# Layer 1 of a four-layer image network: 14 pieces of 224 pixels instead of 19 of 166, and two samples' statistics taken inside it

## The chip, the core and the metric

The kernel runs on one core of one Trainium2 chip. The core has a matrix engine (TensorE, "PE" in the profile, whose weight loads the profile lists apart as "PEld"), a vector engine (DVE), an activation engine (ACT), a general engine (POOL) and a queue engine (SP) that issues transfers. The metric is the device time of one launch in microseconds, as a median of several runs. All data is float32.

## What is computed

The input is 8 images of 128 channels and 56 x 56 = 3136 pixels. Four layers follow each other, each of the form `x = x + layer(groupnorm(x))`. Layer 0 is a windowed attention, layer 2 a masked convolution, layer 3 a residual block of two 3 x 3 convolutions. The change is in layer 1, a recurrent network that walks over the pixels of each image in order:

```python
seq = jnp.transpose(xn, (0, 2, 3, 1)).reshape(B, H * W, C)
inp = tanhshrink(jnp.einsum('blc,ic->bli', seq, w_in) + b_in)
xgate = jnp.einsum('bli,hi->blh', inp, w_ih) + b_ih + b_hh
def step(h, xg):
    h_new = jnp.tanh(xg + h @ w_hh.T)
    return (h_new, h_new)
_, hs = jax.lax.scan(step, h0, xgate_t)
out_seq = jnp.einsum('blh,oh->blo', outputs, w_out) + b_out
```

The sizes are 128 channels, 256 inner inputs (`RIN`), and a state of 512 (`RH`). Layer 2 then needs, for each sample, the mean and variance of every group of 4 channels over all 3136 pixels of layer 1's result, before it can normalise that sample.

## The kernel before

All 8 images stay on the chip in one tile `X` of 128 partitions (channels) by 8 x 3136 pixels. The layers update it in place.

**Layer 1 is cut along the pixels.** The state forgets quickly, so the 3136 steps of a sequence are cut into `NCH` = 19 pieces of `TC` = 166 pixels that advance together: one step handles one pixel of every piece of every image, 19 x 8 = 152 columns. As 19 x 166 = 3154, the first piece is short by `LEAD` = 18 pixels. Each piece begins from the state that its predecessor has at its end, which isn't known at the start. So `WARM` = 56 steps come first, over the last 56 pixels of every piece, from a zero state; the state that they leave, moved on by one piece (`first`, L925 to L930), is where the real run begins. The real run then takes `TC` steps. There are `END = WARM + TC` = 222 steps, issued in pairs by the loop at L906.

**One step** (`step`, L847) does two products per block of 128 state channels, `KH` = 4 blocks. The input product (`wih`) takes 4 x 2 = 8 matmuls, the recurrent one (`whh`) 4 x 4 = 16; all are issued at L858. Each has its own 128 x 128 weights. A float32 matmul leaves two records of a weight load and two of a matmul in the trace, and this document counts records. The result `ps` comes in two halves `f` of two blocks. ACT takes the tanh of each into `hs[f]` (L881). The matmuls of the next step that read `hs[0]` come ahead of those that read `hs[1]`.

**Three phases** follow from that loop:

- warming, 56 steps: input product, recurrent product. The input product of these steps, with its bias, is also copied out of PSUM (`gk`, L870) and stored in DRAM (`kept`, L871).
- main run, `TC` - 56 = 110 steps: input product, recurrent product, and per pair the output product `po` (L893).
- recall, 56 steps: the pixels of the warm steps come again, so their input product isn't computed again but fetched (`recall`, L841), added by DVE (`v`, L884) and given to ACT (L885). These steps have the recurrent product and `po` only.

**Around the steps**, `prepare` (L814) makes the normalised input of a pair of pixels: `xn` on POOL (L822, L826), one product `pi` of two matmuls (L833), tanh on ACT (L835) and `inp` on DVE (L836). `outputs` (L887) forms `po` by four matmuls over a pair of pixels: its first two are issued just ahead of the next pair's first step, its last two ahead of that pair's second step, and then DVE adds the result into `X` (L899). `pi` and `po` work on two pixels at once, thus on 304 columns. The order of the matmuls is written out by hand (a manual schedule of PE); a scheduler places the other engines' work.

**Between the layers.** After the loop POOL compares the states at the seams of the pieces (L936 to L946, into `held`), whose outcome decides at the very end whether layers 1 to 3 are redone by a plain sequential version (L1295; this isn't executed here). In `convolutions` (L953), statistics of sample 0 are seven `bn_stats` over 448 pixels each (L1010) and a `bn_aggr` (L1012); two small products (`pm`, L1016, and `pv`, L1028), a root (L1032) and a reciprocal (L1038) follow, then the normalised image is written into a padded tile (L1040), and `spread` copies it into a tile `g3` by ACT and by transfers on SP and POOL (L1057, L1059). The first product of layer 2 (L1069) reads `g3`. The statistics of sample 1 are one `bn_stats` ahead of that normalisation and six behind it. SP also issues the loads of layer 2's weights there (L982 to L993, L1092), ahead of its share of L1059.

Of the kernel before, what the change touches and what calls it, by code (L numbers as in the profile page):

```python
# [10 lines left out]
F32 = mybir.dt.float32  # L11
# [3 lines left out]
ALU = mybir.AluOpType  # L15
# [3 lines left out]
P = 128  # L19
B = 8  # L20
HW = 56
NPX = HW * HW
# [4 lines left out]
BLK = NW * WPX  # L27
NBLK = NPX // BLK
# [3 lines left out]
KI, KH = RIN // P, RH // P  # L32
PW = HW + 2
EPS = 1e-5
NCH = 19
TC = 166
LEAD = NCH * TC - NPX
WARM = 56
CL = P // 4
VECTORS = (("gamma", 1), ("beta", 1), ("b_in", KI), ("b_ih", KH), ("b_hh", KH), ("b_out", 1))  # L40
# [4 lines left out]
def conv_stack_kernel(ctx: ExitStack, tc: tile.TileContext, a: dict, out: bass.AP):  # L45
# [3 lines left out]
    nc = tc.nc  # L49

    const = ctx.enter_context(tc.tile_pool(name="const", bufs=1))
# [5 lines left out]
    X = xpool.tile([P, B, NPX], F32, name="X")  # L57
# [10 lines left out]
    for b in range(2, B):  # L68
        nc.sync.dma_start(X[:, b, :], a["x"][b])
    mv1 = const.tile([P, B, 2], F32, name="mv1")  # L70
    root = const.tile([P, 1], F32, name="root")
    vecs = const.tile([P, 14], F32, name="vecs")
    eps = const.tile([P, 1], F32, name="eps")
# [44 lines left out]
    broken = keep.tile([1, 1], I32, name="broken")  # L118
    held = keep.tile([P, KH * (NCH - 1) * B // 16], F32, name="held")
    between = ExitStack()  # L120
    samp = between.enter_context(tc.tile_pool(name="samp", bufs=2))
    with ExitStack() as l0:
# [35 lines left out]
        for i in range(3):  # L158
            t = c0.tile([P, WS, PW], F32, name=f"vrow{i}", tag=f"vrow{i}")
# [10 lines left out]
        qs, ks, selrs, v3s, lepes, os_, st1, norms = {}, {}, {}, {}, {}, {}, {}, {}  # L170
# [378 lines left out]
        stats, mean, var = measure(0)  # L549
# [54 lines left out]
        for b in range(1, B):  # L604

            at = [FIRST + i // 4 for i in range(NBLK)] if b == 1 else [pair_of(b - 2, 0) + i for i in range(NBLK)]
# [6 lines left out]
            at = [pair_of(b - 1, i * NW) - 6 for i in range(NBLK)]  # L613
            if b == 1:
                at = [max(t, 2 + 2 * i) for i, t in enumerate(at)]
# [15 lines left out]
        for p in range(FIRST, END + 6):  # L631
            ready = [t for t in jobs if t[1] <= p and all(placed.get(k, p) < p for k in t[7])]
            light, long = (next((t for t in ready if t[5] == k), None) for k in (LIGHT, LONG))
            ready = [t for t in ready if t[5] == ONE]
# [36 lines left out]
        with tc.manual_schedule(engines={ET.PE, ET.Activation, ET.DVE, ET.Pool}):  # L671
            for p in range(FIRST, END + 6):
# [12 lines left out]
                for W in (2 * p - 2, 2 * p - 1):  # L685
                    b, w = divmod(W, NWIN)
# [49 lines left out]
    with ExitStack() as l1:  # L736
# [5 lines left out]
        at = np.cumsum([0] + [n for _, n in VECTORS])  # L742
        gamma, beta, bin_, bih, bhh, bout = (vecs[:, lo:hi] for lo, hi in zip(at, at[1:]))
# [16 lines left out]
        t = c1.tile([P, B], F32, name="t1")  # L760
# [16 lines left out]
        scl = keep.tile([P, B], F32, name="scl")  # L777
        nc.vector.tensor_scalar(scl, r, rb, None, ALU.mult)
        ctr = keep.tile([P, B], F32, name="ctr")
# [6 lines left out]

        pre.close()  # L790
        fast = ExitStack()
        row = fast.enter_context(tc.tile_pool(name="row", bufs=2))
# [2 lines left out]

        def pieces(t):

            c = 0 if t >= LEAD else 1
            at = c * TC + t - LEAD
            return c, X[:, :, at : at + (NCH - 1 - c) * TC + 1 : TC].rearrange("p b c -> p c b")  # L800

        kept = dram.tile([WARM, P, KH, NCH, B], F32, name="kept")

        def pixel(s):

            return TC - WARM + s if s < WARM else s - WARM

        def known(s):

            return s - TC if s >= TC else None  # L810

        seam = row.tile([P, KH, NCH - 1, B], F32, name="seam", bufs=1)

        def prepare(s):  # L814

            xn = row.tile([P, 2, NCH, B], F32, name=f"xn_{s}", tag="xn")
            engine = nc.gpsimd if s else nc.vector
            for t in range(2):
                c, src = pieces(pixel(s) + t)
                if c:  # L820
                    engine.memset(xn[:, t, :c], 0.0)
                engine.tensor_tensor(  # L822
                    xn[:, t, c:], src,
                    ctr.rearrange("p (o b) -> p o b", o=1).broadcast_to((P, NCH - c, B)), ALU.subtract,
                )
                engine.tensor_tensor(  # L826
                    xn[:, t, c:], xn[:, t, c:],
                    scl.rearrange("p (o b) -> p o b", o=1).broadcast_to((P, NCH - c, B)), ALU.mult,
                )
            inp = row.tile([P, KI, 2, NCH, B], F32, name=f"inp_{s}", tag="inp")  # L830
            for m in range(KI):
                pi = ps_a.tile([P, 2, NCH, B], F32, name=f"pi_{s}_{m}", tag="pi")
                nc.tensor.matmul(pi, win_t[:, m * P : (m + 1) * P], xn, start=True, stop=True)  # L833
                th = row.tile([P, 2, NCH, B], F32, name=f"th_{s}_{m}", tag="th")
                nc.scalar.activation(th, pi, AF.Tanh, bias=bine[:, m : m + 1])  # L835
                nc.vector.scalar_tensor_tensor(  # L836
                    inp[:, m], pi, bine[:, m : m + 1], th, ALU.add, ALU.subtract,
                )
            return inp
# [47 lines left out]
        def outputs(s, hs):  # L887

            po = ps_a.tile([P, 2, NCH, B], F32, name=f"po_{s}", tag="po")

            def part(ks):
                for k in ks:
                    nc.tensor.matmul(po, wout[:, k, :], hs[k // 2][:, :, k % 2], start=(k == 0), stop=(k == KH - 1))  # L893

            def end():
                part((2, 3))
                for t in range(2):
                    c, dst = pieces(pixel(s) + t)
                    nc.vector.scalar_tensor_tensor(dst, po[:, t, c:], bout, dst, ALU.add, ALU.add)  # L899

            return [lambda: part((0, 1)), end]

        with tc.manual_schedule(engines={mybir.EngineType.PE}):
            END = WARM + TC
            x, prev, todo = prepare(0), None, []
            for s in range(0, END, 2):  # L906
                hs = [row.tile([P, 2, 2, NCH, B], F32, name=f"hs{f}_{s}", tag=f"hs{f}", bufs=3) for f in range(2)]
                for t in range(2):
                    if known(s) is not None:
                        x = recall(s + t)  # L910


                    if todo:
                        todo.pop(0)()
                    step(s + t, x, hs if t else prev, hs)
                    if t == 0 and s + 2 < END and known(s + 2) is None:
                        nxt = prepare(s + 2)
                if pixel(s) + 2 == LEAD and s >= WARM:
                    for f in range(2):
                        nc.gpsimd.memset(hs[f][:, 1, :, 0, :], 0.0)  # L920
                x, prev = nxt, hs
                if s >= WARM:
                    todo = outputs(s, hs)
                if s + 2 == WARM:
                    first = [row.tile([P, 2, 2, NCH, B], F32, name=f"first{f}", tag=f"hs{f}", bufs=3) for f in range(2)]  # L925
                    for f in range(2):
                        nc.vector.tensor_copy(first[f][:, 1, :, 1:, :], hs[f][:, 1, :, : NCH - 1, :])
                        nc.gpsimd.memset(first[f][:, 1, :, 0, :], 0.0)
                        nc.gpsimd.tensor_copy(seam[:, 2 * f : 2 * f + 2], hs[f][:, 1, :, : NCH - 1, :])
                    prev = first  # L930
            for part in todo:
                part()

# [17 lines left out]
    def convolutions(held=None):  # L953

        with ExitStack() as l2:
            c2 = l2.enter_context(tc.tile_pool(name="c2", bufs=1))
            few = l2.enter_context(tc.tile_pool(name="few", bufs=2))
# [43 lines left out]
            class Norm:  # L1001


                def __init__(self, b, name):
                    self.b, self.name = b, name
                    self.mv = few.tile([P, 2], F32, name=f"mv_{name}", tag="mv2", bufs=3)
                    self.st = few.tile([P, NBLK, 6], F32, name=f"st_{name}", tag="st2")

                def stats(self, i):
                    nc.vector.bn_stats(self.st[:, i, :], X[:, self.b, i * BLK : (i + 1) * BLK])  # L1010
                    if i == NBLK - 1:
                        nc.vector.bn_aggr(self.mv, self.st.rearrange("p i s -> p (i s)"))  # L1012

# [119 lines left out]

            ET = mybir.EngineType
            weights, verdict = [], None
            norms = [Norm(b, f"l2_{b}") for b in range(2)]
            with ExitStack() as order:
                if held is not None:
                    order.enter_context(tc.manual_schedule(engines={ET.PE, ET.Activation, ET.DVE, ET.Pool}))
# [14 lines left out]
                for n in range(B * NBLK):  # L1154
                    b, i = divmod(n, NBLK)
# [86 lines left out]
            def prepare(b):  # L1242

                end = {}
                mv = small.tile([P, 2], F32, name=f"mv3_{b}", tag="mv")

                def norm():
                    gm, r = group_norm(b, ps_g, "pg", f"l3_{b}", mv)
                    nc.vector.tensor_scalar(
                        pad3[:, 1 : 1 + HW, 1 : 1 + HW], X[:, b, :].rearrange("p (u v) -> p u v", v=HW),  # L1250
                        gm, r, ALU.subtract, ALU.mult,
                    )
                    end.update(shift(b, gm, r))

                half = HW // 2
                sums = lambda y: column_sums(va, slice(1 + y, 1 + y + half), pad3[:, 1 + y : 1 + y + half, :])
                stats = lambda: channel_stats(b, mv, f"l3_{b}")
                return end, [stats, norm, lambda: sums(0), lambda: sums(half)]
# [258 lines left out]
```

## Time and profile before

| | us |
|---|---|
| median of 3 runs (3682.0 to 3686.88) | 3684.55 |
| the profiled execution's own time | 3677.05 |
| its span | 3675.1 |
| PE busy (share of the span) | 3545.7 (96%) |
| PE weight loads busy | 2914.9 (79%) |
| DVE busy | 1889.8 (51%) |
| ACT busy | 1654.2 (45%) |
| POOL busy | 1349.3 (37%) |
| first and last recurrent or input matmul of layer 1 begin at (L858) | 1408.9 and 2933.2 |

The span runs from the first to the last instruction of the profiled execution; the 1.95 us around it are launch and end. The profiled execution was 7.5 us faster than the median of the runs. A line of the profile that names a group gives the source line, the engine, the operation, the tile written and those read, the shapes and the count, then the busy time and the mean duration of one. Busy time counts overlapping instructions once, so it is less than count times duration where they are pipelined.

### The profile page before, as it was taken

Reading aid. Unit: us, or ns where it says so; the run is one execution under the profiler, and the core shown is the slowest. Engines: PE = TensorE matmul, PEld = TensorE weight load, DVE = VectorE, ACT = ScalarE, POOL = GpSimd, SP = SyncE. Lnnn points to the kernel's source line nnn. Section 1 sums busy time; section 2 is a strip of 40 time slices with the busy share of each in tenths; the row PEclk is TensorE's granted clock in tenths of the full one; section 3 lists DMA queues with packets and bytes.
Section 4 is the critical chain, followed back from the end, with each engine's and each line's share of the span. In section 5 each row is a group of like instructions: output and inputs, shape, how many; then the busy total and the mean of one; then the engine's idle time right before and its main releaser. Section 6 shows DMA issues by size and latency. Waiting matters only on the chain.

```text
span 3675.1 us, 85966 instructions
## 1 busy us (share of the span) xinstructions
PE 3545.7 (96%) x30150; PEld 2914.9 (79%) x30150; DVE 1889.8 (51%) x3923; ACT 1654.2 (45%) x5149; POOL 1349.3 (37%) x3663
## 2 busy tenths in 40 slices
PE   5999999999999998999999999999999989999998
PEld 3666666666666667999999999999999833799998
DVE  5888888888878773222111111111122266757665
ACT  2787878888888883222222222222211154122222
POOL 3767667676766662111111111111000066323221
PEclk8999999999999999999999999999999999999999
DMA  5444444343434431111000000000022166100000
GB/s 208 108 107 108 110 104 107 100 117 101 118 102 114 122 93 57 49 45 49 21 1 1 1 1 1 1 1 1 18 59 59 45 168 169 34 23 23 31 21 34
DMA packets 195814, 241.74 MB, mean 66 GB/s; under 512 B 42480, under 2 KB 153520, under 8 KB 194352
## 3 DMA queue, kind: packets, MB, share of 16 engines
q1 hardware_dynamic: 160992, 125.99, 11.8%
q0 software_dynamic: 32576, 109.48, 11.3%
q8 instruction: 245, 4.01, 0.5%
q14 instruction: 193, 1.58, 0.2%
q10 hardware_dynamic: 1808, 0.68, 0.1%
HBM read 135.64 MB, written 69.39 MB: 56 GB/s over the span
## 4 chain that ended last, share of the span: by engine, by line
PE 84%; DVE 6%; ACT 4%; issue 3%; DMA 1%; POOL 1%; SPq 0%; DVEq 0%; ACTq 0%; POOLq 0%
PE ps L858 32%; PE pt L497 8%; PE pc3b L1221 7%; PE pc3a L1221 7%; PE s L461 5%; PE po L893 5%; PE po L516 4%; PE plep L375 3%; ACT e L474 3%; PE pc L1069 3%; PE pi L833 2%; DVE nmax L469 2%; PE pq L345 1%; PE pk L253 1%; PE pc L1077 1%
## 5 line engine op out<-in xcount | busy, mean ns | idle before, releaser
L858 PE MATMUL ps<-hs,w_gates 128*128 128x152 f32 x7040 | 948.0, 293 | 0.2 <-DVE gk L870 0.2
L858 PEld LDWEIGHTS ps<-hs,w_gates 128*128 128x128 f32 x7040 | 924.9, 190 | 8.3 <-issue 0.4
L474 ACT ACTIVATE e<-s,nmax 128x256 f32<-128x256 f32 x1568 | 732.3, 480 | 250.4 <-DVE nmax L469 246.7
L881 ACT ACTIVATE hs<-ps,bg 128x152 f32<-128x152 f32 x664 | 221.3, 384 | 932.2 <-PE ps L858 923.0
L836 DVE SCALAR_TENSOR_TENSOR inp<-pi,bine,th 128x304 f32<-128x304 f32 x166 | 83.0, 533 | 854.5 <-ACT th L835 854.5
L469 DVE TENSOR_REDUCE nmax<-s 128x2 f32<-128x512 f32 x784 | 501.0, 680 | 22.7 <-PE s L461 22.7
L497 PEld LDWEIGHTS pt<-c_ident,e 128*128 128x128 f32 x3136 | 353.1, 141 | 191.4 <-issue 103.0
L497 PE MATMUL pt<-c_ident,e 128*128 128x128 f32 x3136 | 450.6, 279 | 29.4 <-ACT e L474 10.2
L822 POOL TENSOR_TENSOR xn<-X,ctr 128x152 f32<-128x152 f32 (+1 forms) x164 | 92.1, 581 | 898.1 <-PE pi L833 893.6
L858 PEld LDWEIGHTS ps<-inp,w_gates 128*128 128x128 f32 x2656 | 363.4, 191 | 19.6 <-DVE inp L836 1.6
L858 PE MATMUL ps<-inp,w_gates 128*128 128x152 f32 x2656 | 372.8, 294 | 0.3 <-DVE inp L836 0.2
L474 ACT ACTIVATION_READ_ACCUMULATOR e<-s,nmax 128x1 f32 x1568 | 323.0, 206 | 0.0
L436 POOL COPY ks<-kT 128x64 f32 x1568 | 300.2, 237 | 17.8 <-PE s L461 12.0
L485 POOL TENSOR_TENSOR rc<-rden,c_own 128x128 f32<-128x128 f32 x392 | 148.4, 399 | 394.1 <-DVE rden L482 249.6
L499 DVE COPY eT<-pt 128x512 f32<-128x512 f32 x392 | 263.0, 671 | 19.6 <-PE pt L497 11.5
L1221 PE MATMUL pc3b<-vb,u_w2c_t 128*128 128x224 f32 x1344 | 257.6, 353 | 0.0
L1221 PE MATMUL pc3a<-va,u_w1c_t 128*128 128x224 f32 x1344 | 255.6, 353 | 1.4 <-DVE va L1211 1.4
L1221 PEld LDWEIGHTS pc3a<-va,u_w1c_t 128*128 128x128 f32 x1344 | 254.2, 190 | 1.5 <-POOL va L1210 1.5
L1221 PEld LDWEIGHTS pc3b<-vb,u_w2c_t 128*128 128x128 f32 x1344 | 253.6, 190 | 0.0
L461 PE MATMUL s<-ks,qm 32*128 32x256 f32 x3136 | 250.9, 403 | 0.1
L500 ACT COPY eT<-pt 128x512 f32<-128x512 f32 x392 | 235.8, 602 | 4.9 <-PE pt L497 3.6
L516 PE MATMUL po<-eT,vs 128*32 128x128 f32 x6272 | 226.4, 277 | 12.0 <-ACT eT L500 10.6
(224 smaller groups left out, 4400.2 us busy)
## 6 DMA issues: line engine op xcount, KB each, us to landing
vs<-vpix SPq DMA_DIRECT2D x1568, 32.0 KB, 2.1
kept<-gk SPq DMA_DIRECT2D x56, 304.0 KB, 2.1
g<-kept SPq DMA_DIRECT2D x56, 304.0 KB, 2.7
v<-vimg POOLq DMA_DIRECT2D x56, 290.0 KB, 4.0
v<-vimg POOLq DMA_DIRECT2D x56, 289.5 KB, 4.9
v<-vimg POOLq DMA_DIRECT2D x56, 289.0 KB, 5.8
vimg<-vrow POOLq DMA_DIRECT2D x56, 232.0 KB, 2.8
X<-in_x_dram SPq DMA_DIRECT2D x8, 1568.0 KB
```

What stands on the lines that cost most here:

```text
L436: nc.gpsimd.tensor_copy(kw[:, t : t + 1, :], ks[b][:, bass.ds(idx[t], 1), :])
L461: nc.tensor.matmul(s_["s"][g][:, o, :], w["qm"][h].rearrange("p h x -> p (h x)"), w["kw"][h], start=True, stop=True,)
L469: nc.vector.tensor_reduce(s_["nmax"][:, g, :], s_["s"][g], AX.X, ALU.max, negate=True)
L474: nc.scalar.activation(wins[2 * p + o]["e"][:, g, :], s_["s"][g][:, o, :], AF.Exp, bias=s_["nmax"][:, g, o : o + 1], accum_out=s_["den"][: ...
L497: nc.tensor.transpose(pt[c][:, g, :], s_["e"][:, g, c * P : (c + 1) * P], ident)
L499: nc.vector.tensor_copy(s_["eT"][0], pt[0])
L500: nc.scalar.copy(s_["eT"][1], pt[1])
L516: nc.tensor.matmul(po[ch, o, 0], s_["vw"][:, c, ch], s_["eT"][c][:, g, :], start=(c == 1), stop=(c == 0),)
L858: nc.tensor.matmul(ps[f][:, i], w, src, start=(i == 0 and k == 0 and h != fresh), stop=(k == KH - 1 if h else k == KI - 1 and (s < WARM or ...
L881: nc.scalar.activation(hs[f][:, s % 2, i], ps[f][:, i], AF.Tanh, bias=bg[:, m : m + 1])
L893: nc.tensor.matmul(po, wout[:, k, :], hs[k // 2][:, :, k % 2], start=(k == 0), stop=(k == KH - 1))
L1221: nc.tensor.matmul(m[k], u[:, dy, k, :], v[:, k, i * WS + dy : i * WS + dy + WS, :], start=(dy == 0), stop=(dy == 2),)
```

## The change

- `NCH` = 14 and `TC` = 224. As 14 x 224 = 3136, all pieces are equal: `LEAD` is gone, and with it the zeros written for the short piece and the narrower forms of `xn` and of the addition into `X`. `WARM` stays at 56. There are now 56 + 224 = 280 steps of 14 x 8 = 112 columns: 56 warming, 168 of the main run, 56 of recall. `pi` and `po` have 224 columns.
- Statistics of layer 2's samples 0 and 1 are begun in layer 1. A block of 448 values is no longer a run of pixels but 32 pixels (`CHUNK`) of all 14 pieces. As soon as all pieces are 32 pixels further, one `bn_stats` for each of the two samples is issued, into a lasting tile `st2`. The seventh block of sample 0 follows the last addition into `X`; that of sample 1 and both `bn_aggr` stay where layer 2 has its statistics.
- The other samples, and the version that redoes layer 1, take statistics as before.

```diff
-NCH = 19
-TC = 166
-LEAD = NCH * TC - NPX
+NCH = 14
+TC = 224
+CHUNK = BLK // NCH
 WARM = 56
...
+    st2 = const.tile([P, 2, NBLK, 6], F32, name="st2")
...
         def pieces(t):
-            c = 0 if t >= LEAD else 1
-            at = c * TC + t - LEAD
-            return c, X[:, :, at : at + (NCH - 1 - c) * TC + 1 : TC].rearrange("p b c -> p c b")
+            return X[:, :, t : t + (NCH - 1) * TC + 1 : TC].rearrange("p b c -> p c b")
+
+        def stats(b, j):
+            cols = X[:, b, :].rearrange("p (c t) -> p c t", t=TC)[:, :, j * CHUNK : (j + 1) * CHUNK]
+            nc.vector.bn_stats(st2[:, b, j, :], cols)
...
             for t in range(2):
-                c, src = pieces(pixel(s) + t)
-                if c:
-                    engine.memset(xn[:, t, :c], 0.0)
                 engine.tensor_tensor(
-                    xn[:, t, c:], src,
+                    xn[:, t], pieces(pixel(s) + t),
...
-                if pixel(s) + 2 == LEAD and s >= WARM:
-                    for f in range(2):
-                        nc.gpsimd.memset(hs[f][:, 1, :, 0, :], 0.0)
+                if ready:
+                    stats(*ready.pop(0))
+                if s > WARM and pixel(s) % CHUNK == 0:
+                    ready += [(b, pixel(s) // CHUNK - 1) for b in range(2)]
...
+            assert not ready
+            stats(0, NBLK - 1)
...
-                def __init__(self, b, name):
-                    self.b, self.name = b, name
+                def __init__(self, b, name, known=0):
+                    self.b, self.name, self.known = b, name, known
...
+                    self.st = st2[:, b] if known else few.tile([P, NBLK, 6], F32, name=f"st_{name}", tag="st2")
                 def stats(self, i):
...
+                    if i >= self.known:
+                        nc.vector.bn_stats(self.st[:, i, :], cols)
                     if i == NBLK - 1:
                         nc.vector.bn_aggr(self.mv, self.st.rearrange("p i s -> p (i s)"))
...
-            norms = [Norm(b, f"l2_{b}") for b in range(2)]
+            known = NBLK - 1 if held is not None else 0
+            norms = [Norm(0, "l2_0", known and NBLK), Norm(1, "l2_1", known)]
```

More of the change, by code (lines that the diff above doesn't have):

```diff
@@ L818, in prepare @@
             for t in range(2):
-                c, src = pieces(pixel(s) + t)
-                if c:
-                    engine.memset(xn[:, t, :c], 0.0)
                 engine.tensor_tensor(
-                    xn[:, t, c:], src,
-                    ctr.rearrange("p (o b) -> p o b", o=1).broadcast_to((P, NCH - c, B)), ALU.subtract,
+                    xn[:, t], pieces(pixel(s) + t),
+                    ctr.rearrange("p (o b) -> p o b", o=1).broadcast_to((P, NCH, B)), ALU.subtract,
                 )
                 engine.tensor_tensor(
-                    xn[:, t, c:], xn[:, t, c:],
-                    scl.rearrange("p (o b) -> p o b", o=1).broadcast_to((P, NCH - c, B)), ALU.mult,
+                    xn[:, t], xn[:, t],
+                    scl.rearrange("p (o b) -> p o b", o=1).broadcast_to((P, NCH, B)), ALU.mult,
                 )
@@ L897, in end @@
                 for t in range(2):
-                    c, dst = pieces(pixel(s) + t)
-                    nc.vector.scalar_tensor_tensor(dst, po[:, t, c:], bout, dst, ALU.add, ALU.add)
+                    dst = pieces(pixel(s) + t)
+                    nc.vector.scalar_tensor_tensor(dst, po[:, t], bout, dst, ALU.add, ALU.add)
             return [lambda: part((0, 1)), end]
@@ L904, in conv_stack_kernel @@
             END = WARM + TC
-            x, prev, todo = prepare(0), None, []
+            x, prev, todo, ready = prepare(0), None, [], []
             for s in range(0, END, 2):
@@ L1001, in convolutions @@
             class Norm:
-                def __init__(self, b, name):
-                    self.b, self.name = b, name
+                def __init__(self, b, name, known=0):
+                    self.b, self.name, self.known = b, name, known
                     self.mv = few.tile([P, 2], F32, name=f"mv_{name}", tag="mv2", bufs=3)
-                    self.st = few.tile([P, NBLK, 6], F32, name=f"st_{name}", tag="st2")
+                    self.st = st2[:, b] if known else few.tile([P, NBLK, 6], F32, name=f"st_{name}", tag="st2")
                 def stats(self, i):
-                    nc.vector.bn_stats(self.st[:, i, :], X[:, self.b, i * BLK : (i + 1) * BLK])
+                    if self.known:
+                        cols = X[:, self.b, :].rearrange("p (c t) -> p c t", t=TC)
+                        cols = cols[:, :, i * CHUNK : (i + 1) * CHUNK]
+                    else:
+                        cols = X[:, self.b, i * BLK : (i + 1) * BLK]
+                    if i >= self.known:
+                        nc.vector.bn_stats(self.st[:, i, :], cols)
                     if i == NBLK - 1:
```

## The prediction

> **What bounds the kernel now.** I read the page's chain of what ended last first. TensorE holds 84% of it, and the matmuls of layer 1's steps (L858) alone hold 32% of the span; with L893 and L833 it is 39%.
>
> ```profile
> PE 84%; DVE 6%; ACT 4%; issue 3%; DMA 1%; POOL 1%; SPq 0%; DVEq 0%; ACTq 0%; POOLq 0%
> ```
>
> So the price of a matmul record decides. Next came the same chain in order of time (start, us, what, number of records). The reader is to divide: in the main run 48 records of 152 columns take 6.20 us, 129.2 ns each; four of 304 columns take 1.02 us, 255.5 ns each; layer 3's 168 of 224 columns take 31.78 us, 189.2 ns each.
>
> ```profile
> 1429.37 12.50 PE ps L858 x96
> ...
> 2606.22 6.20 PE ps L858 x48
> 2641.29 4.13 PE ps L858 x32
> ...
> 3186.64 31.78 PE pc3b L1221 x168
> ```
> ```profile
> 2202.97 1.02 PE po L893 x4
> ```
>
> These three lie on one line: 0.83 ns per column and 3 ns per record. Carried down to 112 columns it gives 96 ns. But it says nothing of narrow records, so I looked for narrow matmuls with full weights. Two groups of layer 0 have them, in the timeline (start, us, engine, group, count): L306 with 49 columns and L285 with 128.
>
> ```profile
> 188.03 0.52 PEld L306 LDWEIGHTS pw<-xm,wqkv 128*128 128x128 f32 x4 [0.71 <-ACT lep L382]
> 188.03 0.65 PE L306 MATMUL pw<-xm,wqkv 128*128 128x49 f32 x4 [0.47 <-ACT lep L382]
> ```
> ```profile
> 243.18 0.97 PEld L285 LDWEIGHTS pvp<-wqkv,xw 128*128 128x128 f32 x8 [0.33 <-DVE eT L499]
> 243.18 1.16 PE L285 MATMUL pvp<-wqkv,xw 128*128 128x128 f32 x8
> ```
>
> A weight load lasts 190 ns there, and loads overlap; the first of a row to the last is the busy time less one duration. L306: (520 - 190) / 3 = 110 ns from load to load, although 49 columns would stream in some 44 ns. L285: (970 - 192) / 7 = 111 ns. So loads follow each other no closer than about 110 ns, and a narrow record pays that. In layer 1 the load is hidden now: 110 ns under 129.
>
> Last, a pair of recall steps in the timeline. The loads of `po` wait 0.31 us for ACT: the path from the last matmul of half 0 over DVE's `v` and ACT's tanh is longer than the eight records of half 1 that cover it.
>
> ```profile
> 2907.54 4.30 PE L858 MATMUL ps<-hs,w_gates 128*128 128x152 f32 x32
> ...
> 2910.90 0.47 DVE L884 TENSOR_TENSOR v<-ps,g 128x304 f32<-128x304 f32 x1 [2.28 <-issue]
> 2911.41 0.46 ACT L885 ACTIVATE hs<-v 128x304 f32<-128x304 f32 x1 [3.65 <-DVE v L884]
> 2911.91 0.81 PEld L893 LDWEIGHTS po<-hs,xw 128*128 128x128 f32 x4 [0.31 <-ACT hs L885]
> ```
>
> [...] The larger of the two prices should hold.
>
> **The change part by part.**
>
> *Steps.* Narrow records (L858). Before: 55 pairs of the main run and 28 warming pairs at 96, 28 recall pairs at 64, less 32 that the first step lacks: 9728 (the page counts 7040 + 2656, and 32 read `first`). After: 84 and 28 pairs at 96, 28 at 64, less 32: 12512. Before they cost 9728 x 0.1292 = 1256.9 us. After, at 0.110 us each, 1376.3 us. The unknown is bounded below by streaming, 0.096, and above by 0.112, since L285 and L306 show 109 to 112 by the duration of the load before it (189 to 192 ns; L858's last 190). I take 0.110.
>
> *Wide records* (L833, L893). Before 332 + 664 = 996 at 0.2555 = 254.5 us. After 28 x 4 + 84 x 12 + 28 x 8 = 1344, with 224 columns at 0.1892 = 254.3 us. No change.
>
> *The wait in recall.* Before, a pair takes 10.66 us, of which the records make 64 x 0.1292 + 8 x 0.2555 = 10.31: 0.35 x 28 = 9.8 us. The path was 8 x 0.129 + 0.35 = 1.38 us. With 80 columns fewer, DVE saves some 0.08 (it does about one column per ns by the rows of 152 and 304), ACT 0.07 (384 ns at 152, 515 at 304), the matmul 0.02: 1.2 us. The cover is 8 x 0.110 = 0.88. The wait stays at about 0.35, 9.9 us.
>
> *The same wait in the main run.* There the first `po` matmul needs only the first block's tanh, 0.29 + 0.04 + 0.39 + 0.03 = 0.75 us after half 0 ends, under 1.03. After: about 0.70 under 0.88. I count nothing; if the tanh came 0.4 later, each of 84 pairs would pay 0.2.
>
> *Warming.* Its pairs carry 0.1 us of semaphore records (57 of 51 ns), 2.9 us, kept.
>
> Before, that sums to 1256.9 + 254.5 + 9.8 + 2.9 = 1524.1 us, against 1527.0 from the first matmul at 1408.9 to the end of the last `po` at 2935.9, so the account misses 3 us of start. After: 1376.3 + 254.3 + 9.9 + 2.9 = 1643.4. Layer 1 grows by 119.3 us.
>
> *Other engines in the steps.* DVE, ACT and POOL were busy 1.9, 3.5 and 2.1 us of a main pair's 15.47; with narrower forms and a pair of some 12.8 us they stay far below TensorE. Transfers of `kept` shrink from 304 to 224 KB, at the same number and a recall pair of 8.9 us. The zeros that go (105 ns on POOL, 9 pairs) were hidden.
>
> *Statistics in layer 1.* Twelve `bn_stats` of about 0.54 us (3.78 for seven, below) between the steps. Ten fall into the main run on an idle DVE. Two are queued in recall ahead of one `v`; behind that waits ACT, then TensorE, but DVE is idle for 2.3 us before that `v` now (the 2.28 of the fence above). I count 0. That they read 14 strided runs isn't shown for `bn_stats`; at twice the price (1.1 us each) it would cost at most 1 us once.
>
> *Start of layer 2.* In the timeline seven `bn_stats` run in a row once `X` is complete; six of them go, 3.24 us of DVE.
>
> ```profile
> 2936.86 3.78 DVE L1010 BATCH_NORM_STATS2 st_l<-X 128x6 f32<-128x448 f32 x7
> ...
> 2940.53 0.26 POOL L945 TENSOR_TENSOR held<-seam 128x36 f32<-128x36 f32 x1
> ...
> 2940.82 0.34 SPq L982 DMA_DIRECT2D w<-in_w_c_dram  x1
> ...
> 2945.52 10.18 SPq L1059 DMA_DIRECT2D g<-pad  x15
> ```
>
> What is late next is SP: it begins its loads at 2940.82, when POOL has finished the seams, and comes to the copies of `g3` only at 2945.52, though their image was there from about 2944. Earlier statistics don't move SP; the seams do, being 104 columns for 144: of their 6 us about 1 goes. So 1 us is gained (between 0 and 3.24). Sample 1's six later `bn_stats`, 3.25 us from 2947.07, go too, but lie beside the waits for these copies: 0.
>
> Sum: +119.3 - 1 = +118.3 us, 3677.05 to 3795.4 for the profiled execution, and 3684.55 to 3802.9 for the median, as the profiled one was 7.5 below it.
>
> **The rivals.**
>
> *Columns set the price.* Column-steps fall from 222 x 152 to 280 x 112, by 7%. If loads hid further than L306 shows, since TensorE has long queues of them here and only four there, a record would cost 0.096: 12512 x 0.096 + 254.3 + 28 x 0.47 + 2.9 = 1471.5, with layer 2's 1 us a gain of 53.6: 3631 us, faster. The point that decides is 100.5 ns a record: below it the change gains. Against it speak eight loads in a row at 111 ns, where the queue could have run ahead too. Chance 0.05.
>
> *The recurrence becomes the bound.* Half 1's cover shrinks from 1.03 to 0.88 us while the fixed latencies of DVE and ACT stay. If a main pair then waits 0.2 us and a recall pair 0.7 instead of 0.35, that adds 17 + 10 us: 3830. For it speaks that recall waits already; against it the 0.18 us of room in the main run. Chance 0.12.
>
> *The loads get dearer than in L285*[...]: 0.115 would add 63 us, 3865. Nothing shows it, the load rows of L858 last 190 as elsewhere. Chance 0.03.
>
> **How the numbers follow.** The forecast has 0.80: 3803 us. Its own range is that of the load's price: 0.002 us x 12512 = 25 us either way. With the second rival's 3830 at the upper end I give 3780 to 3832; the first and third lie outside. A difference under 0.2% (7 us) can't be told from no change. Faster 0.05, within 0.2% 0.01, slower 0.94.
>
> **What would show it.** L858's records of 112 columns should lie 110 ns apart in the chain (48 of them in 5.28 us), a main pair should take 12.8 us, a recall pair 8.9, and layer 1 should last some 1646 us. 96 ns would make the first rival right. Waits of `po` for `hs` in the main run would show the second. `bn_stats` ahead of `v` with TensorE idle would show that the statistics cost. Layer 2's first product should follow the last `po` after about 14 us instead of 15.

## The result and the profile after

The changed kernel takes 3812.6 us (3811.67 to 3814.43, 4 runs) where the kernel before takes 3683.28 us in 4 runs: a ratio of 1.0355 (95% interval 1.0337 to 1.0373), 3.5% slower. The forecast was 3803 us in a range of 3780 to 3832. The profiled execution took 3811.67 us (span 3809.5), 134.6 us more than the one before.

From the page after, the two groups of the recurrent product (line, engine, operation, shapes, count, then busy time and mean duration of one):

```profile
L858 PE MATMUL ps<-hs,w_gates 128*128 128x112 f32 x8896 | 1041.1, 275 | 0.2 <-DVE gk L870 0.2
L858 PEld LDWEIGHTS ps<-hs,w_gates 128*128 128x128 f32 x8896 | 1019.7, 192 | 2.3 <-issue 0.4
```

They were 7040 records, 948.0 us for matmuls and 924.9 us for loads. Busy time per matmul record fell from 135 to 117 ns only, for 26% fewer columns. That the loads are busy as long as the matmuls says nothing: they were before, because one of 190 ns overlaps the next even when they start 129 ns apart. The spacing counts, and the chain in order of time gives it:

```profile
1601.15 10.93 PE ps L858 x96
...
2604.86 5.34 PE ps L858 x48
```

48 records in 5.34 us: 111.3 ns from record to record (129.2 before). The chain also holds the period of a pair of the main run, 2604.86 to 2617.85: 12.99 us, as against 15.47. Layer 1, from its first matmul to the end of its last `po`, lasts 1670.4 us (1406.9 to 3077.2); it was 1529.5 by the same measure (1406.4 to 2935.9). This measure begins with the first product `pi`, some 2 us ahead of the matmul that the prediction begins with.

Who waited for whom in the main run, 1800 to 2600 us, longest first (total us, times, longest):

```profile
DVE inp L836 <- ACT th L835: 707.6, 62, 11.5
POOL xn L822 <- PE pi L833: 702.0, 62, 11.3
ACT hs L881 <- PE ps L858: 609.7, 246, 4.7
```

TensorE isn't in this list. In recall it waits, as before; a pair, 3021.42 to 3030.40, takes 8.98 us, and `po` still waits for the tanh, 0.25 us as the load's idle time shows it (0.31 before):

```profile
3021.42 0.68 PEld L893 LDWEIGHTS po<-hs,xw 128*128 128x128 f32 x4 [0.25 <-ACT hs L885]
...
3030.40 0.68 PEld L893 LDWEIGHTS po<-hs,xw 128*128 128x128 f32 x4 [0.25 <-ACT hs L885]
```

At the start of layer 2, in the timeline (the lines that answer to those of before: statistics, SP's first load, SP's copies of `g3`, then the first product and the load of layer 3's first weights):

```profile
3078.05 0.63 DVE L803 BATCH_NORM_STATS2 st<-X 128x6 f32<-128x448 f32 x1
...
3081.24 0.34 SPq L986 DMA_DIRECT2D w<-in_w_c_dram  x1
...
3085.49 14.41 SPq L1069 DMA_DIRECT2D g<-pad  x15
...
3088.36 7.00 PE L1079 MATMUL pc<-g,w 96*32 96x448 f32 x48 [7.38 <-DMA g<-pad]
...
3099.94 0.59 SPq L1102 DMA_DIRECT2D t_w1c_t<-in_w1c_t_dram  x1
```

One `bn_stats` for seven. But there is something that the diff doesn't say: `t_w1c_t`, 590 KB of weights for layer 3, was issued by SP at 2944.99, ahead of its copies of `g3` (2945.52); now it comes at 3099.94, behind those of sample 0. The scheduler moved it. The lines of before, with the first product:

```profile
2944.99 0.43 SPq L1092 DMA_DIRECT2D t_w1c_t<-in_w1c_t_dram  x1
...
2950.86 5.58 PE L1069 MATMUL pc<-g,w 96*32 96x448 f32 x30 [7.76 <-DMA g<-pad]
```

From the end of the last `po` to the first product of layer 2 it is 11.1 us (14.9 before), and from there to the first product of layer 3 200.2 us (203.8): 7.4 us less, where the forecast had 1.

So of 134.6 us, layer 1 gives +140.9 and the stretch behind it -7.4; the rest, 1 us, is spread over layers 0 and 3.

### The profile page after: what moved, and what is told of

Read it like the earlier page. It is cut to its first block, busy times and chain, and to the rows that moved or that the text cites. A ratio compares the mean times of both kernels' runs of the same rounds, so it can differ in the third digit from the quotient of the medians.

```text
span 3809.5 us, 92842 instructions
## 1 busy us (share of the span) xinstructions
PE 3684.3 (97%) x33282; PEld 3123.9 (82%) x33282; DVE 1885.7 (49%) x4039; ACT 1698.6 (45%) x5439; POOL 1364.3 (36%) x3759
## 4 chain that ended last, share of the span: by engine, by line
PE 86%; DVE 5%; ACT 4%; issue 2%; DMA 1%; POOL 0%; SPq 0%; ACTq 0%; DVEq 0%; POOLq 0%
PE ps L858 35%; PE pt L498 7%; PE pc3b L1232 7%; PE pc3a L1232 7%; PE s L462 5%; PE po L893 5%; PE po L517 4%; PE pc L1079 4%; PE plep L376 3%; ACT e L475 3%; PE pi L833 2%; DVE nmax L470 1%; PE pc L1087 1%; PE pq L346 1%; PE pk L254 1%
## 5 line engine op out<-in xcount | busy, mean ns | idle before, releaser
L858 PE MATMUL ps<-hs,w_gates 128*128 128x112 f32 x8896 | 1041.1, 275 | 0.2 <-DVE gk L870 0.2
L858 PEld LDWEIGHTS ps<-hs,w_gates 128*128 128x128 f32 x8896 | 1019.7, 192 | 2.3 <-issue 0.4
L881 ACT ACTIVATE hs<-ps,bg 128x112 f32<-128x112 f32 x896 | 268.7, 351 | 1070.9 <-PE ps L858 1063.1
L836 DVE SCALAR_TENSOR_TENSOR inp<-pi,bine,th 128x224 f32<-128x224 f32 x224 | 90.8, 446 | 1053.6 <-ACT th L835 1053.6
L822 POOL TENSOR_TENSOR xn<-X,ctr 128x112 f32<-128x112 f32 x222 | 100.5, 475 | 1190.7 <-PE pi L833 1186.3
L858 PE MATMUL ps<-inp,w_gates 128*128 128x112 f32 x3584 | 435.7, 275 | 0.3 <-DVE inp L836 0.3
L858 PEld LDWEIGHTS ps<-inp,w_gates 128*128 128x128 f32 x3584 | 434.7, 192 | 1.1 <-DVE inp L836 1.1
```

The source lines that it names most:

```text
L858: nc.tensor.matmul(ps[f][:, i], w, src, start=(i == 0 and k == 0 and h != fresh), stop=(k == KH - 1 if h else k == KI - 1 and (s < WARM or ...
L881: nc.scalar.activation(hs[f][:, s % 2, i], ps[f][:, i], AF.Tanh, bias=bg[:, m : m + 1])
```

## The experiments

Two questions: does the weight load set the price of a record, or columns, or a floor of another kind, or the recurrence; and where do the 7.4 us of layer 2 come from? Ratios are to runs of the kernel before on the same chip (3677 to 3678 us there). The expectations count from 3683 us, so the distance to the kernel before is what is compared, not the time itself.

**Half the weight columns.** The upper 64 channels of every block of the state are left out; records, columns and order stay. The results `ps` lie in fixed places here, so that their unwritten half is zero.

```diff
...
-            ps = [ps_r.tile([P, 2, NCH, B], F32, name=f"ps_{s}_{f}", tag=f"ps{f}") for f in range(2)]
+            ps = fixed[s % 2]
...
+            W = P // 2
...
-                        w = whh[:, k, m * P : (m + 1) * P] if h else wih[:, k, m * P : (m + 1) * P]
+                        w = whh[:, k, m * P : m * P + W] if h else wih[:, k, m * P : m * P + W]
...
-                            ps[f][:, i], w, src,
+                            ps[f][:W, i], w, src,
```

> The changed kernel with only the first 64 of each 128 weight columns loaded in the steps (L858), so that the upper 64 channels of every block of the state are left out; number of records, 112 moving columns and waits stay. If the weight load sets the price of a record (112 ns now), a load of half the columns falls below the 96 ns of streaming and the record costs 96: 12512 x 0.0156 = 195 us less, some 6 us given back in recall, where the cover of the tanh shrinks: about 3623 us. If a record has a floor of 112 ns of its own, whatever it loads, the time stays at 3813 us. If the recurrence is the bound, it stays too.

Measured: 3705.38 us, 1.0074 times before (1.0059 to 1.009), 28 us above the kernel before. The load's price has 60 below it, the two others 130 above. That lies between, so the trace decides. In the timeline of a main step (L864 and L899 are L858 and L893 of the changed kernel):

```profile
2301.54 0.68 PEld L899 LDWEIGHTS po<-hs,xw 128*128 128x128 f32 x4
2301.54 1.02 PE L899 MATMUL po<-hs,xw 128*128 128x224 f32 x4
...
2302.50 1.53 PEld L864 LDWEIGHTS ps<-inp,w_gates 128*64 128x64 f32 x16 [0.28 <-issue]
2302.50 1.75 PE L864 MATMUL ps<-inp,w_gates 128*64 128x112 f32 x16
2303.99 3.11 PEld L864 LDWEIGHTS ps<-hs,w_gates 128*64 128x64 f32 x32
2304.08 3.23 PE L864 MATMUL ps<-hs,w_gates 128*64 128x112 f32 x32
```

32 records in 3.23 us, the last one lasting 0.26: (3.23 - 0.26) / 31 = 96 ns. With a load of half the columns, the same 112 columns cost the 96 ns of streaming. A floor of 112 ns per record, whatever it loads, is excluded, and so is the recurrence as the bound. The edit halves the channels of the result together with the load, so it doesn't separate the load from a price that would go with the result's channels; no run here does.

What the expectation missed is the idle 0.28 us ahead of 2302.50: wherever weights of 64 columns follow weights of 128, or the reverse, time is lost. By the starts of the matmuls a group of `pi` or `po` pays about 93 ns on entering, 105 for its second record and 93 on leaving, 73 us over 252 groups. Other gaps between records of the steps come to 26 us, where the changed kernel has 8. Layer 1 lasts 1562.5 us, 108 less than in the changed kernel. The price of a record alone gives 195, and less 73 and 18 that is 104.

**Fewer columns, same records.** Two pieces of each image are left out of layer 1; their pixels pass through it unchanged.

```diff
-NCH = 14
+NCH = 12
 TC = 224
-CHUNK = BLK // NCH
+CHUNK = 32
```

> The changed kernel with the last two of the 14 pieces of each image left out of layer 1 (their pixels pass through it unchanged): 96 moving columns, the same number of steps and records. If the weight load sets the price, the narrow records stay at 112 ns and only the wide ones fall, from 189 to about 163 ns: 1344 x 0.027 = 36 us less, about 3777 us. If columns set it, 16 fewer at 0.83 ns on 12512 records take another 166 us: about 3610 us.

Measured: 3768.77 us, 1.0253 (1.0237 to 1.0268), 92 us above the kernel before. The load's price has 94 above it, the columns' price 73 below. The chain:

```profile
2012.61 5.33 PE ps L858 x48
2018.62 5.33 PE ps L858 x48
```

5.33 us for 48: 111.0 ns at 96 columns, 111.3 at 112. Sixteen columns more cost 0.3 ns a record, where streaming at 0.83 ns per column would add 13. Up to where they stream as long as a load takes, columns are all but free here.

**More columns.** Two kernels on the other side of that point.

```diff
-NCH = 14
-TC = 224
+NCH = 16
+TC = 196
```

> The changed kernel with 16 equal pieces of 196 pixels (blocks of 28 pixels of all pieces): 128 columns, 252 steps. The price of a record is the larger of its load, 111.6 ns, and its streaming, 109.2: 11168 narrow records at 0.1118 = 1249 us, 1176 wide ones at 0.2158 = 254 us, 13 us of waits: 1515 us against 1524 by the same account before. With some 7 us less at layer 2, where the load of the first convolution weights again stands behind the copies of g3: 16 us faster than before, about 3667 us where before has 3683. If the equal pieces or the statistics had a cost of their own that the price per record doesn't explain, it would show as a time above 3675.

Measured: 3665.03 us, 0.9964 (0.995 to 0.9977), 13 us faster than before where 16 were expected. Its chain:

```profile
2017.49 5.36 PE ps L858 x48
```

111.7 ns at 128 columns. Layer 1 lasts 1524.8 us, 4.7 less than before, not the 9 of the account. About what is missing is a wait in the warming phase that the account left out: the first recurrent record follows 198 ns after the last input record there, 86 more than a record takes, over 56 steps 4.8 us. (In the kernel before it follows after 129 ns, without a wait.)

And the kernel before, unequal pieces, with 17 of them:

```diff
-NCH = 19
-TC = 166
+NCH = 17
+TC = 186
```

> The kernel before with 17 pieces of 186 pixels, the first short by 26; all else as before. 136 columns lie just above the load: streaming 115.8 ns. 10688 narrow records at 0.1158 = 1238 us, 1116 wide ones at 0.2292 = 256 us, 13 us of waits: 1506 us, 18 us less than before, about 3665 us where before has 3683. If the time fell with the column-steps alone, 242 x 136 for 222 x 152, 2.5% of 1250 us would go: 31 us less, 3652 us.

Measured: 3661.16 us, 0.9953 (0.9939 to 0.9966), 17 us faster, as the price per record says (18) and not the column-steps (31). Layer 1 itself lasts 1517.7 us, 11.8 less than before where 18 were expected; the same wait in the warming phase (174 ns where a record takes 116) makes 3 us of the difference, and the rest was not traced. So some 5 us of the 17 come from layer 2, whose length varies from run to run (199.7 us here, 203.8 before).

```profile
2048.62 5.56 PE ps L858 x48
```

115.8 ns at 136 columns. The five widths give one picture: 111.0, 111.3, 111.7, 115.8 and 129.2 ns at 96, 112, 128, 136 and 152 columns, the larger of load and streaming each time (by 0.83 ns per column plus 3, 128 columns would stream in 109, an estimate).

**The load of layer 3's weights.** First the changed kernel without its statistics in layer 1:

```diff
-                if ready:
-                    stats(*ready.pop(0))
-                if s > WARM and pixel(s) % CHUNK == 0:
-                    ready += [(b, pixel(s) // CHUNK - 1) for b in range(2)]
...
-            stats(0, NBLK - 1)
...
-            known = NBLK - 1 if held is not None else 0
+            known = 0
```

> 14 pieces alone; all statistics of layer 2 are taken in layer 2, as before the change. Layer 1 should last the same 1670 us in both theories. Theory that the changed kernel's gain at layer 2 comes from where the load of the first convolution weights stands in SP's queue (it stands ahead of the first copies of g3 again here): layer 2 loses 6 us, about 3819 us. Theory that the statistics themselves gave it, by freeing DVE: 7 us, about 3820 us. The two are told apart by the next run, not by this one.

Measured: 3814.59 us, 1.0372 (1.0358 to 1.0386), 138 us above the kernel before where both theories have 136 to 137. Layer 1 lasts 1671.9 us, as long as with the statistics: they cost nothing there. Then the statistics kept and the load put ahead of the copies:

```diff
+                weights.append(transformed("w1c_t"))
                 for c in range(5):
                     norms[0].normal([c])
                     spread(0, c)
...
-                    if i == 0 and b in (1, 3):
+                    if i == 0 and b == 3:
```

> The changed kernel, statistics in layer 1 included, with the load of the first convolution weights (t_w1c_t, 590 KB) put ahead of the copies of g3 in SP's queue, where it stood before the change. If that order gave the gain, the first product of layer 2 comes 13.6 us after the last output product of layer 1 instead of 11.1, and layer 2 lasts 203.8 us instead of 200.2: 6 us more, about 3819 us. If the statistics gave it by freeing DVE, nothing changes: 3813 us.

Measured: 3816.01 us, 1.0373 (1.0359 to 1.0388), 139 us above the kernel before, where the order of the load has 136 and the statistics 130. The timeline:

```profile
3081.70 3.12 DVE L1050 TENSOR_SCALAR pad<-X,gm_l,r_l 128x504 f32<-128x504 f32 x5
...
3085.43 0.45 SPq L1102 DMA_DIRECT2D t_w1c_t<-in_w1c_t_dram  x1
3085.97 13.18 SPq L1069 DMA_DIRECT2D g<-pad  x15
...
3093.16 6.68 PE L1079 MATMUL pc<-g,w 96*32 96x448 f32 x31 [11.98 <-DMA g<-pad]
```

SP's first copy is issued at 3085.97, half a microsecond later than in the changed kernel, but the first product comes 7.2 us behind it instead of 2.9: 15.9 us after the last `po`. Layer 2 itself lasts 200.0 us, not the 203.8 expected. So the load's place counts at the start of layer 2, and the length of the rest has another cause or varies.

The opposite, in the kernel before, by a tiny write that the load waits for (the function loads both of layer 3's weights, so the second gets the write too):

```diff
+                nc.vector.memset(w[:, 0, 0:1], 0.0)
                 nc.sync.dma_start(w, a[name])
```

> The kernel before, with one tiny DVE write into the tile of the first convolution weights ahead of their load, so that SP issues it behind the copies of g3 of both first samples. If that order is worth what the trace of the load-first run says, layer 2 ends 4 to 6 us earlier: about 3678 us where before has 3683. If the changed kernel's gain at layer 2 came from the statistics, nothing changes: 3683 us.

Measured: 3675.8 us over 21 runs, 0.9992 (0.9986 to 0.9999): 2 to 3 us faster, less than the 4 to 6 expected. First product 11.8 us after the last `po` (14.9 before), layer 2 203.5 us.

Three runs on one chip then set both parts apart: the pieces alone with the late load (the edit that takes the statistics out of layer 1 and the tiny write together), the changed kernel again, and the load-first kernel again.

> 14 pieces, all statistics of layer 2 in layer 2, and the load of the first convolution weights behind the copies of g3, by a tiny DVE write into its tile. Beside the changed kernel on the same chip it tells what the statistics in layer 1 give when the load is out of the way in both. If the load's place is what counted at layer 2: within 2 us of the changed kernel, as SP comes to the copies of g3 about when the image is ready. If the six statistics taken off the chain count: their 3.2 us slower than the changed kernel.

> The changed kernel again, for comparison with the runs beside it on the same chip: 1.0355 times the kernel before.

> The load-first run again, beside the changed kernel on the same chip: 3 to 6 us slower than it if the load's place counts, the same if not.

Measured: changed kernel 3810.24 us, load first 3813.79, late load without the statistics 3815.55 (1.0359, 1.0369 and 1.0374; each interval about 0.0014 either way, so that their overlap leaves the 3.6 us between the first two open by the ratios alone). The last is 5.3 us above the changed kernel, more than either theory of its expectation has. The traces say how it comes about. In the kernel without the statistics:

```profile
3078.52 3.78 DVE L1015 BATCH_NORM_STATS2 st_l<-X 128x6 f32<-128x448 f32 x7
...
3085.28 3.12 DVE L1045 TENSOR_SCALAR pad<-X,gm_l,r_l 128x504 f32<-128x504 f32 x5
3086.11 10.83 SPq L1064 DMA_DIRECT2D g<-pad  x15
...
3089.12 9.96 PE L1074 MATMUL pc<-g,w 96*32 96x448 f32 x48 [4.37 <-DMA g<-pad]
```

The image is begun at 3085.28, 7.6 us after the last `po`; in the changed kernel it is 4.3 us. Its first product comes early enough, but 48 records of it take 9.96 us, with gaps for copies, as against 7.00. Counted from the end of the last `po` record to the start of the 49th record of layer 2, in us:

| | load ahead of the copies | load behind them |
|---|---|---|
| statistics in layer 2 (19 pieces) | 23.7 | 21.3 |
| statistics in layer 2 (14 pieces) | 23.8 | 21.6 |
| statistics in layer 1 (14 pieces) | 24.6 and 24.2 | 18.3 and 18.4 |

Two values are two executions. The tiny write puts the load 44 to 47 us after the last `po`, behind the copies of both first samples; in the changed kernel it stands at 22.7, behind those of the first alone. The statistics alone give nothing, the load alone gives 2, both together give 5.4. The later of the two, image or copies, sets the start: while the load delays the copies, an earlier image gains nothing, and once the load is behind them the six statistics are worth 3.2 us, what they last on DVE (3.24). In the full timings, taking away either half costs 3.6 or 5.3 us; what goes beyond the start lies in the rest of layer 2.

**Both together.** 17 pieces and the late load:

> 17 pieces of 186 and the late load of the first convolution weights together: the two gains lie in different stages and should add, 18 + 5 = 23 us: about 3660 us where before has 3683.

Measured: 3659.93 us, 0.9943 (0.9929 to 0.9956), faster than before by 18 us in the medians and 21 by the ratio, where 23 were expected. It has the lowest median of these runs, but it is only 1.2 us below the 17 pieces alone and the intervals overlap, so that the late load adds anything here isn't shown by the times.

## Why the prediction was right, and where its terms were off

**The price of a record** was the step that carried the result, and it held: 111.3 ns for the 110 taken, within the 109 to 112 read off L285 and L306. 12512 x 0.0013 = 16 us of the forecast's error is this. The rival of streaming, 96 ns and 3631 us, is refuted, and with half-width weights the 96 ns do appear, so the 111 ns go with the 128 weight columns.

That loads follow each other no closer than about 110 ns holds only for rows of 128 x 128 loads: in layer 0's transposes (L497 before), 287 loads start 56 to 65 ns after the one before, which was in each case the first behind a pause (232 ns or more), and the next then follows at 109 to 113 in 266 of the cases. The streaming line, 0.83 ns per column and 3 ns per record, was read at 152, 224 and 304 columns; carried down it gives estimates of 116 ns at 136 columns and 96 at 112, and the runs with 17 pieces and with half the weights have 115.8 and 96. That the larger of the two prices holds is what the five widths show.

**The wide records** cost a little more than said: a main pair's 12.99 us less 2 x 5.34 leaves 2.31 us for 12, 192 ns for 189, over 1344 some 4 us. The excess lies in the second record of each group (205 ns); the others take 189.

**The waits.** In recall a pair took 8.98 us for 8.9 expected; with the dearer records taken off, 0.32 us of it is the wait, for 0.35, over 28 pairs 1 us less. In the main run there was none, so the second rival is refuted too. Left out was a wait in the warming phase: its steps add the recurrent product onto `ps` after DVE has copied it out (`gk`), and the eight records that cover that copy have become shorter:

```profile
1606.46 1.95 PE L858 MATMUL ps<-inp,w_gates 128*128 128x112 f32 x16
...
1607.55 0.58 DVE L870 TENSOR_SCALAR gk<-ps,bg 128x112 f32<-128x112 f32 x2 [4.02 <-PE ps L858]
...
1608.28 0.45 PE L858 MATMUL ps<-hs,w_gates 128*128 128x112 f32 x2
```

By the starts of the matmuls the first recurrent record follows, in the mean, 161 ns after the last input record where a record takes 112 (129 for 129 before): 0.05 x 56 = 3 us. That the copy is what it waits for is read from these lines and from how the excess grows with the columns copied: 10, 49 and 86 ns with 12, 14 and 16 pieces. The profile names the copy as what ended 0.2 us of such gaps; most are too short for it to name anything.

Together 16 + 4 + 3 - 1 = 22 us (records, wide records, warming, recall), and layer 1 measured +140.9 for +119.3.

**The statistics in layer 1** cost nothing, as counted: 1670.4 us with them and 1671.9 without. Each of the 13 took 627 ns (median) over its 14 runs of 32 pixels; the double price that was kept as a bound isn't there. A single one over a run of pixels took as long before:

```profile
2942.38 0.62 DVE L1010 BATCH_NORM_STATS2 st_l<-X 128x6 f32<-128x448 f32 x1
```

**The start of layer 2** is the step that was mis-sized: 1 us (0 to 3.24) for 7.4. It named what was late next, SP, and SP did come to the copies earlier by about the 1 us foreseen: 8.3 us after the end of the last `po` for 9.6. But it took the rest as fixed. From SP's first copy to the first product 5.3 us passed before and 2.9 after, as the 590 KB no longer stand ahead. By the 49th record the gain is 5.4 us; the other 2 lie in the length of the rest of layer 2, which ran from 197.4 to 203.8 us over the profiled executions of the kernels here, and which no run ascribes to one cause.

So the profiled execution grew by 134.6 us for 118.3 expected, as two errors, +22 in layer 1 and -6 behind it, partly cancelled, and 1 us came from other layers. That the medians are closer to the forecast, 3812.6 for 3803, is luck: the profiled execution lies only 1 us under its median now, not the 7.5 that the forecast carried over.

## What to carry to other kernels

In layer 1 of this kernel, where every float32 matmul brings 128 weight columns of its own, the price of a record is the larger of two lines: 111 to 112 ns at 96, 112 and 128 columns, and 0.83 ns per column plus 3 at 136 and 152. Only the sloping one is seen while the columns are many; before cutting columns, look in the same trace for a narrow matmul with full weights to find the flat one. By these figures the lines cross near 131 columns, an estimate. Of the cuts run, layer 1 is shortest with the one just above that (17 pieces, 1517.7 us; 16 take 1524.8, 19 take 1529.5; 18 were not run), since fewer pieces also repeat fewer pixels for warming. And where two things gate a stage, taking one off the chain shows only once the other has been moved as well; the scheduler did that here unasked, so compare the built order of every queue, not the diff alone.

## What was not expected of the hardware

- Where records with 64 weight columns follow records with 128, or the reverse, time is lost: 0.28 us idle ahead of the first load of 64, some 290 ns per change there and back, though loads of 64 in a row left the spacing at the 96 ns of streaming. The runs don't show why.
- `bn_stats` over 448 values in 14 strided runs took 627 ns, about what a single one took over 448 in a row (0.62 us before).
